# Attention by tiles: six polynomial exps per group instead of five, their squares on GpSimd, and the loads of the next group in another order

## The chip, the cores and the metric

The kernel runs on one NeuronCore of a Trainium2 chip. Its engines work side by side, each through its own instructions in order: TensorE (PE; its weight loads are listed as PEld), VectorE (DVE), ScalarE (ACT), GpSimd (POOL) and SyncE (SP), which here only issues DMA transfers. The metric is the device time of one execution in microseconds (us), as a median over runs.

## The reference

A graph network of four layers on 3327 nodes of width 128. Everything that is changed here lies in the first layer, an attention with 128 heads of width 8 over all pairs of nodes, with the adjacency matrix added twice as a bias:

```python
q = (x @ Wq.T).reshape(d, n, h)      # d = 128 heads, n = 3327 nodes, h = 8
k = (x @ Wk.T).reshape(d, n, h)
v = (x @ Wv.T).reshape(d, n, h)
a = jnp.einsum('dnh,dmh->dnm', q, k) * scale
a = a + spatial_encoding + edge_encoding          # both are adj
a = jax.nn.softmax(a, axis=2)
out = jnp.einsum('dnm,dmh->dnh', a, v)
```

So 128 x 3327 x 3327 exponentials are taken, 1.4 thousand million. The other three layers multiply the same adjacency matrix by matrices of width 128; the change does not touch them.

## The kernel before, in words

**Tiling.** Scores stand transposed, keys on the partitions. The queries are cut into 7 chunks `c` of 476 (the last 472); the 128 heads into 32 groups `g` of 4; the keys into 26 tiles of 128, taken two by two as 13 pairs `q`. One *pair* `u` is thus (chunk, group, pair of key tiles): 7 x 32 x 13 = 2912 pairs in 224 groups, and each pair makes 4 heads x 2 key tiles = 8 tiles of 128 x 476 scores.

**Steps.** The loop `for i in range(-4, 4 * n + 15)` has four steps to a pair. At step i ScalarE's exp of one head (`exps(u, j)`) stands: head j of pair u comes at i = 4u + 3j, so that four pairs are in flight. At every odd i TensorE gets a *batch*: the scores of the heads due at steps i + 1 and i + 2 (two key tiles each, so 4 matmuls, L654), then four heads' products with the values for one key tile (`values`, L713; each is two matmul instructions in the profile, so 8). So there are two batches to a pair and 26 to a group.

**Scores in place.** A score tile keeps its PSUM bank for all four heads. VectorE first writes adj - shift into it (`seed`, L645); TensorE adds head 0's scores; ScalarE reads exp(2 x) of it (L666 both key tiles at once, 952 columns, or L669 one of 476 where the two banks aren't neighbours); then TensorE adds k1 q1 - k0 q0, and so on. For that `QS` holds, for each head, its q beside the negated q of the head before. The seven banks of `S` go round, so a seed must wait until ScalarE has read the fourth head of the pair that held the bank before.

**Exps by hand.** In the pairs with q in `BY_HAND = (0, 2, 5, 7, 10)`, VectorE makes the exp of head 0's second key tile in place of ScalarE. This tile isn't seeded: its matmul starts the bank with the bare product. `hand_exp` scales it into `h` (L691), seeds the bank for head 1, and then evaluates a polynomial in three steps (L695) and a last one that multiplies by `EA` = exp(2 (adj - shift)) (L697). `EA` is made once per chunk for each q of `BY_HAND` by a subtraction (L678) and a ScalarE exp (L683). The steps of this generator are drawn one by one in the main loop, and `heads_of` lets the product with the values of such a tile come one pair later.

**Loads.** In pair q = 1 of each group the SP queue gets the 16 transfers of the next group's keys (`load_k`, L551), the 6 of its first q (`load_q`, L562 and L564), and the values (`load_v`, L575). At q = 3, 5, 7 GpSimd negates a q over all 128 partitions (L570), and the next q is loaded over half of that (6 transfers; 9 for head 1, which is also wanted in `QZ`). At q = 8 GpSimd spreads the values into `VA` (L580) and runs `all_here` (L584), a copy that reads a column of every key row; the first scores of the next group wait for it. At most eight SP transfers are outstanding, because the ninth waits for the semaphore of the first.

**Beside it.** adj for later chunks is transposed behind the attention in 22 squares of 128 rows; each takes four groups for loading (L283, q = 0), two half turns on VectorE (L288, q = 4 and 9) and a row maximum (L292, q = 12), and in a fifth group its maxima go out and back through HBM (`gather` at q = 0, L299; `back` at q = 1, L304), a bound is formed (q = 7) and 1.66 MB of transposed adj are stored (`store`, L295, q = 8). GpSimd also carries the four stores of each group's result (L725), which wait for VectorE's copy (L721).

**Start of the stage.** The SP queue gets the first values, keys, first q, shift, other q's, and then the 26 tiles of adj.

Of the kernel before, what the change touches and what calls it, by code (L numbers as in the profile page):

```python
# [10 lines left out]
F32 = mybir.dt.float32  # L11
# [6 lines left out]
ALU = mybir.AluOpType  # L18
# [4 lines left out]
P = 128  # L23
N = 3327
D = 128
H = 8
HD = D * H
NT = 26
NP = NT * P
NQ = NT // 2  # L30
# [6 lines left out]
CW = 476  # L37
# [8 lines left out]
NOTHING = -1.0e30  # L46


EXP_C = (0.9999990463256836, 2.2162604331970215, 2.4563632011413574, 1.8291265964508057)
EXP_ARG = 0.9023826718330383  # L50
BY_HAND = (0, 2, 5, 7, 10)
LN_EPS = 1e-5
L1_EPS = 1e-7
L1_MAX_TANH = 1.0 - 1e-6
# [34 lines left out]
def gnn_kernel(ctx: ExitStack, tc: tile.TileContext, x, adj, Wq, Wk, Wv, Wo, embed, layer,  # L89
               embed_bias, layer_bias, weight, bias, W_in, W_out, out):  # L90
    nc = tc.nc
# [14 lines left out]
    kS_d = dram.tile([2, H, HEADS, NP], F32, name="kS_d")  # L106
# [418 lines left out]
    with tc.tile_pool(name="e1", bufs=1) as e1, tc.tile_pool(name="e_adj", bufs=28) as e_adj, \  # L525
# [12 lines left out]
        S = e_ps.tile([P, 7, 512], F32, name="S")  # L538
        po = e_ps.tile([P, 512], F32, name="po")

        def load_k(c, g):

            b = (c * NG + g) % 2
            for j in range(4):
                d = 4 * g + j
                k0, nk = max(0, j - 1), 1 if j in (0, 3) else 2
                for r in range(2):
                    r0 = 64 * r + 32 * (1 - j % 2)
                    k_d = kS_d[:, :, d, r * NQ * P:(r + 1) * NQ * P].rearrange("i e n -> (i e) n")
                    for i in range(2):  # L550
                        nc.sync.dma_start(KT[b][r0 + 16 * i:r0 + 16 * i + 16, k0:k0 + nk, :].bitcast(F32),  # L551
                                          k_d.unsqueeze(1).to_broadcast([16, nk, NQ * P]))

        def load_q(c, g, j):

# [11 lines left out]
        def negate_q(c, g, j):  # L567

            b, w = (c * NG + g) % 2, width_of(c)
            nc.gpsimd.tensor_scalar(QS[b][:, j + 1, :w], QS[b][:, j, :w].bitcast(F32),  # L570
                                    -1.0, 0.0, op0=ALU.mult, op1=ALU.add)

        def load_v(c, g):
            v = e2.tile([P, 4, NT * H], F32, name="VR", bufs=1)
# [24 lines left out]
        with tc.If(loose < 1), tc.manual_schedule():  # L599
# [39 lines left out]
            def bank(u, r):  # L639
                return S[:, banks(u)[r], :width_of(pairs[u][0])]  # L640
# [19 lines left out]

            def exps(u, j):
                w, (even, odd) = width_of(pairs[u][0]), banks(u)
                e = e_of[u, j] = e_e.tile([P, 2, CW], F32, name=f"e{j}", bufs=(5, 4, 3, 2)[j])
                hand = j == 0 and by_hand(u)
                if even > odd and not hand:
                    touch(u, (0, 1), nc.scalar.activation(e[:, :, :w], S[:, odd:even + 1, :w], AF.Exp, scale=2.0))  # L666
                    return
                for r in range(1 if hand else 2):
                    touch(u, [r], nc.scalar.activation(e[:, 1 - r, :w], bank(u, r), AF.Exp, scale=2.0))  # L669

            def by_hand(u):

                return 0 <= u < n and pairs[u][2] in BY_HAND

            def shifted(c, q):

                w = width_of(c)
                nc.vector.tensor_tensor(EA[q][:, :w], adj_of[c][2 * q + 1][:, :w], shift_of[c][:, :w], op=ALU.subtract)  # L678

            def bare(c, q):  # L680

# [3 lines left out]
            def hand_exp(u):  # L685


                w = width_of(pairs[u][0])
                s = e_h.tile([P, CW], F32, name="h")[:, :w]
                e = e_of[u, 0][:, 0, :w]  # L690
                touch(u, [1], nc.vector.tensor_scalar(s, bank(u, 1), EXP_ARG, None, op0=ALU.mult))  # L691
                seed(u, 1)
                yield
                for k in (3, 2, 1):
                    nc.vector.scalar_tensor_tensor(e, s if k == 3 else e, EXP_C[k], s, op0=ALU.add, op1=ALU.mult)  # L695
                    yield
                nc.vector.scalar_tensor_tensor(e, e, EXP_C[0], EA[pairs[u][2]][:, :w], op0=ALU.add, op1=ALU.mult)  # L697

            def heads_of(u, r):


                first = (u, r)
                if by_hand(u) and r == 1:
                    first = (u + 1, 0)
                elif by_hand(u - 1):
                    first = (u, 1) if r == 0 else (u - 1, 1)
                return [first] + [(u, r)] * 3

            def values(u, r):
                c, g, q = pairs[u]  # L710
                w, k = width_of(c), c * NG + g
                for j, (v, of) in enumerate(heads_of(u, r)):
                    nc.tensor.matmul(po[32 * j:32 * j + H + 1, :w], VA[k % 2][:, 2 * pairs[v][2] + of, j, :],  # L713
                                     e_of[v, j][:, 1 - of, :w], start=(q == 0 and r == 0),
                                     stop=(q == NQ - 1 and r == 1))

            def store(u):
# [9 lines left out]
            def loads(u):  # L727

                c, g, q = pairs[u]
                k = c * NG + g  # L730
                if k + 1 < NC * NG:
                    nxt = divmod(k + 1, NG)
                    if q == 1:
                        load_k(*nxt)
                        load_q(*nxt, 0)
                        v_of[k + 1] = load_v(*nxt)
                    if q in (3, 5, 7):
                        negate_q(*nxt, q // 2 - 1)
                        load_q(*nxt, q // 2)
                    if q == 8:  # L740
                        spread_v(*nxt, v_of.pop(k + 1))
                        here[k + 1] = all_here(*nxt)
                if c + 1 < NC and (g, q) == (0, 0):
                    plan_squares(c)
                if g == NG - 1 and c + 1 < NC:
                    if q == 0:
                        shift_of[c + 1] = load_shift(c + 1)
                        adj_of[c + 1] = []
                    while len(adj_of[c + 1]) < min(NT, 2 * q + 6):
                        adj_of[c + 1].append(load_adj(c + 1, len(adj_of[c + 1])))  # L750


# [2 lines left out]
            def plan(u, f, *a):  # L755
                behind.setdefault(u, []).append((f, a))

            def plan_squares(c):
                for k, s in enumerate(range(squares_of(c), squares_of(c + 1))):
                    sq, u = Square(e_t, s), (c * NG + 7 * k + 1) * NQ  # L760
                    for j in range(4):
                        plan(u, sq.load, j)
                        plan(u + 4, sq.turn, j, 0)
                        plan(u + 9, sq.turn, j, 1)
                        plan(u + 12, sq.largest, j)
                        u += NQ
                    for k, f in ((0, sq.gather), (1, sq.back), (7, sq.finish), (8, sq.store)):
                        plan(u + k, f)

            v0 = load_v(0, 0)  # L770
            load_k(0, 0)
            load_q(0, 0, 0)
            shift_of[0] = load_shift(0)
            for j in range(3):
                negate_q(0, 0, j)
                load_q(0, 0, j + 1)
            spread_v(0, 0, v0)
            here[0] = all_here(0, 0)
            adj_of[0] = [load_adj(0, t) for t in range(NT)]

            for c in range(NC):
                for q in BY_HAND:
# [13 lines left out]
            for i in range(-4, 4 * n + 15):  # L796
                u, j = in_slot(i)
                if 0 <= u < n:
                    exps(u, j)
                at = i % 4  # L800
                if i == -4:
                    seed(0, 0)
                if at == 0 and by_hand(i // 4):
                    by_vector.append(hand_exp(i // 4))
                    next(by_vector[-1])
                for k in range(0 if at % 3 else 1 if at else 0 if by_hand(i // 4) else 2):
                    if by_vector and next(by_vector[0], True):
                        by_vector.popleft()
                if at == 0 and i >= 0:
                    for f, a in behind.pop(i // 4, ()):  # L810
                        f(*a)
                if at == 1 and (i + 3) // 4 < n and not by_hand((i + 3) // 4):
                    seed((i + 3) // 4, 1)
                u = (i - 14) // 4
                if at == 2 and 0 <= u < n and pairs[u][2] == NQ - 1:
                    store(u)
                if at == 2 and (i + 6) // 4 < n:
                    seed((i + 6) // 4, 0)
                if at % 2:
                    for k in (1, 2):  # L820
                        u, j = in_slot(i + k)
                        if 0 <= u < n:
                            scores(u, j)
                    u, r = ((i - 11) // 4, 0) if at == 3 else ((i - 13) // 4, 1)
                    if 0 <= u < n:
                        values(u, r)
                if at == 0 and 0 <= i // 4 < n:
                    loads(i // 4)
# [678 lines left out]
```

## Time and profile before

| | us |
|---|---|
| median of 3 runs | 10980.69 (10976.75 to 10984.85) |
| the profiled execution, whole | 10981.96 |
| the profiled execution, span on the core | 10980.2 |
| first scores of the attention / last product with the values | 461 / 10170 |
| a group of 13 pairs, median of 224 | 43.16 |

In the span from 461 to 10171 us the profile has TensorE busy for 9613.05 us, ScalarE 9669.34, VectorE 7787.13 and GpSimd 1290.03, of 9710; the granted TensorE clock there is 1.00, and the 16 DMA engines are busy for 58%.

How to read it: "busy" is the time in which an instruction of the engine is recorded as running. Successive instructions of ScalarE overlap in the record (a mean of 1099 ns for 952 columns, while they follow each other every 845 ns at best), so a busy ScalarE may still be waiting for part of it. In the rows of groups, the line stands first, then engine, operation, output<-inputs, shapes and count, then busy time and mean duration, then the idle time before them and what ended it. In the timeline each row is a start, a duration, engine, line, operation and count; equal neighbours are merged.

### The profile page before, as it was taken

The numbers are of one execution on the slowest core, as the hardware profiler recorded it, in microseconds if no ns is written. First come the engines' busy times: TensorE is split into PE (matmuls) and PEld (weight loads), VectorE is DVE, ScalarE is ACT, GpSimd is POOL, SyncE is SP. The second block draws the span as 40 slices with busy tenths as digits, with TensorE's granted clock in tenths as the row PEclk, the third lists the DMA queues.
The fourth block names the chain that finished last, engine by engine and source line by source line (L and its number), as shares of the span: only waits on it lengthen the run. The fifth ranks groups of instructions, "written<-read, shape, count | busy, mean of one in ns | idle before, by whom it ended". The sixth has DMA issues, their size and how long they took to land. (4 is left out here: it accounts for less than half of the span.)

```text
span 10980.2 us, 204474 instructions
## 1 busy us (share of the span) xinstructions
PE 10533.5 (96%) x72876; PEld 3435.7 (31%) x72876; DVE 8487.1 (77%) x13503; ACT 10033.1 (91%) x13789; POOL 1529.1 (14%) x2477
## 2 busy tenths in 40 slices
PE   4599999999999999999999999999999999999889
PEld 2133333333333333333333333333323333333544
DVE  5588887888878887788887888878877777777655
ACT  3599999999999999999999999999999999999330
POOL 5011111111111111111111111111111111111101
PEclk7799999999999999999999999999999999999999
DMA  8766566565566565565556565565556555554668
GB/s 250 250 99 97 94 96 113 93 98 96 89 118 97 93 97 88 106 98 97 90 95 119 94 96 93 95 119 95 87 93 98 96 95 86 82 88 71 206 233 281
DMA packets 695339, 1256.98 MB, mean 114 GB/s; under 512 B 195218, under 2 KB 555049, under 8 KB 691244
## 3 DMA queue, kind: packets, MB, share of 16 engines
q1 hardware_dynamic: 644044, 1114.42, 55.7%
q0 software_dynamic: 50272, 129.37, 4.3%
q8 instruction: 587, 9.62, 0.4%
q14 instruction: 436, 3.57, 0.2%
HBM read 1096.53 MB, written 146.60 MB: 113 GB/s over the span
## 5 line engine op out<-in xcount | busy, mean ns | idle before, releaser
L666 ACT ACTIVATE e<-S 128x952 f32<-128x952 f32 (+1 forms) x9024 | 8357.9, 1099 | 36.7 <-PE S L654 29.4
L713 PE MATMUL po<-e,VA 128*9 128x476 f32 (+1 forms) x46592 | 5737.5, 564 | 33.0 <-DVE OS L721 12.3
L645 DVE TENSOR_TENSOR S<-a,shb 128x476 f32<-128x476 f32 (+1 forms) x5824 | 3937.9, 676 | 1447.6 <-ACT e L666 1059.4
L654 PE MATMUL S<-QS,KT 64*128 64x476 f32 (+1 forms) x22176 | 4528.6, 445 | 79.7 <-DMA a<-adjT 28.4
L654 PEld LDWEIGHTS S<-QS,KT 64*128 64x128 f32 x22176 | 2073.7, 184 | 5100.5 <-issue 1301.3
L669 ACT ACTIVATE e<-S 128x476 f32<-128x476 f32 (+1 forms) x4128 | 2467.5, 711 | 1.1 <-PE S L654 0.6
L695 DVE SCALAR_TENSOR_TENSOR e<-e,h 128x476 f32<-128x476 f32 (+1 forms) x2240 | 1497.8, 669 | 77.0
L713 PEld LDWEIGHTS po<-e,VA 128*9 128x9 f32 x46592 | 691.0, 88 | 1606.6 <-issue 1488.1
L570 POOL TENSOR_SCALAR QS<-QS 128x476 fp32r<-128x476 f32 (+1 forms) x672 | 485.6, 723 | 4312.1 <-DMA QS<-qS_d 2612.2
L725 POOL DMA_DIRECT2D oT_d<-OS x896 | 470.5, 530 | 3668.8 <-DVE OS L721 3625.5
L691 DVE TENSOR_SCALAR h<-S 128x476 f32<-128x476 f32 (+1 forms) x1120 | 728.0, 650 | 300.9 <-PE S L654 296.5
L697 DVE SCALAR_TENSOR_TENSOR e<-e,EA 128x476 f32<-128x476 f32 (+1 forms) x1120 | 759.6, 678 | 0.0
L695 DVE SCALAR_TENSOR_TENSOR e<-h 128x476 f32<-128x476 f32 (+1 forms) x1120 | 743.1, 663 | 0.0
L1107 PE MATMUL pu<-strip,y 128*128 128x512 f32 (+2 forms) x1456 | 600.5, 566 | 31.7 <-DVE y L968 14.8
L654 PE MATMUL S<-QZ,KT 64*128 64x476 f32 (+1 forms) x1120 | 493.4, 441 | 11.9 <-DVE S L645 10.5
L1107 PEld LDWEIGHTS pu<-strip,y 128*128 128x128 f32 (+1 forms) x1456 | 271.9, 191 | 305.8 <-issue 272.1
L1111 DVE TENSOR_REDUCE deg<-strip 128x1 f32<-128x1536 f32 (+1 forms) x104 | 193.8, 1881 | 63.7 <-DMA strip<-adjT 44.1
L580 POOL COPY VA<-VR 128x832 f32<-128x832 f32 x224 | 242.3, 1082 | 0.0
L654 PEld LDWEIGHTS S<-QZ,KT 64*128 64x128 f32 x1120 | 205.1, 183 | 92.2 <-DVE S L645 52.4
L288 DVE STREAM_TRANSPOSE cols<-rows 128x416 f32<-128x416 f32 x208 | 204.5, 988 | 30.3 <-DMA rows<-in_adj_dram 22.6
L1060 ACT COPY uT<-pu 128x512 f32<-128x512 f32 (+1 forms) x21 | 11.1, 555 | 222.6 <-PE pu L1107 222.6
L721 DVE COPY OS<-po 128x476 f32<-128x476 f32 (+1 forms) x224 | 146.3, 653 | 87.3 <-PE po L713 87.3
(255 smaller groups left out, 1958.6 us busy)
## 6 DMA issues: line engine op xcount, KB each, us to landing
KT<-kS_d SPq DMA_DIRECT2D x1792, 208.0 KB
KT<-kS_d SPq DMA_DIRECT2D x1792, 104.0 KB
VR<-v_d SPq DMA_DIRECT2D x224, 416.0 KB
QS<-qS_d SPq DMA_DIRECT2D x3072, 14.9 KB
QS<-qS_d SPq DMA_DIRECT2D x1536, 29.8 KB
adjT<-cols SPq DMA_DIRECT2D x26, 1664.0 KB
a<-adjT SPq DMA_DIRECT2D x156, 238.0 KB
strip<-adjT POOLq DMA_DIRECT2D x39, 895.5 KB, 5.1
```

The lines of the kernel that those rows point to most:

```text
L570: nc.gpsimd.tensor_scalar(QS[b][:, j + 1, :w], QS[b][:, j, :w].bitcast(F32), -1.0, 0.0, op0=ALU.mult, op1=ALU.add)
L580: nc.gpsimd.tensor_copy(VA[(c * NG + g) % 2][:, :, :, 0:H], v.rearrange("p j (t e) -> p t j e", e=H))
L645: touch(u, [r], nc.vector.tensor_tensor(bank(u, r), adj_of[c][2 * q + r][:, :w], shift_of[c][:, :w], op=ALU.subtract))
L654: x = nc.tensor.matmul(bank(u, r), KT[b][64 * r:64 * r + 64, max(0, j - 1), q * P:(q + 1) * P], q_s[64 * r:64 * r + 64, :w], start=hand an ...
L666: touch(u, (0, 1), nc.scalar.activation(e[:, :, :w], S[:, odd:even + 1, :w], AF.Exp, scale=2.0))
L669: touch(u, [r], nc.scalar.activation(e[:, 1 - r, :w], bank(u, r), AF.Exp, scale=2.0))
L691: touch(u, [1], nc.vector.tensor_scalar(s, bank(u, 1), EXP_ARG, None, op0=ALU.mult))
L695: nc.vector.scalar_tensor_tensor(e, s if k == 3 else e, EXP_C[k], s, op0=ALU.add, op1=ALU.mult)
L697: nc.vector.scalar_tensor_tensor(e, e, EXP_C[0], EA[pairs[u][2]][:, :w], op0=ALU.add, op1=ALU.mult)
L713: nc.tensor.matmul(po[32 * j:32 * j + H + 1, :w], VA[k % 2][:, 2 * pairs[v][2] + of, j, :], e_of[v, j][:, 1 - of, :w], start=(q == 0 and r ...
L725: nc.gpsimd.dma_start(oT_d[:, d * N + c * CW:d * N + c * CW + w], o[32 * j:32 * j + H + 1, :w])
L1107: nc.tensor.matmul(ps[:, :k], y[:m, t, :], s[:m, c * 4 * P - c0:c * 4 * P - c0 + k], start=(t == 0), stop=(t == NT - 1))
```

## The change

It does five things.

1. `BY_HAND` becomes (0, 2, 4, 6, 8, 10). The polynomial is another one of the same degree: z = s + c0 on VectorE, z z on **GpSimd** (128 x 476, a new line), then z' = (zz + c1) + z, e = (zz + c2) z' and e = (e + c3) EA on VectorE. That is four VectorE instructions and one on GpSimd in place of five on VectorE. The constant that the polynomial leaves out goes into `shifted`.
2. The generator is drawn at other steps: none at step 3 of the pair itself, two at the next step 0, one at the next step 3. `heads_of` is gone: each product with the values comes with its own pair. `e0` has 4 buffers instead of 5.
3. All four q's of the next group are loaded at q = 1, ahead of the keys; the negations write only the two blocks of 32 partitions that hold the q (two instructions of 32 partitions each) and come at q = 5, 7, 9. The values are loaded at q = 3, and spread and `all_here` come at q = 12.
4. Squares: loads at q = 3, turns at q = 10 and 12, `store` at q = 2 of the fifth group (before: q = 8); adj tiles of the next chunk are asked for one pair later.
5. At the start of the stage: the q's, the shift and four tiles of adj, then the keys, the values, and the other 22 tiles.

```diff
-BY_HAND = (0, 2, 5, 7, 10)
+BY_HAND = (0, 2, 4, 6, 8, 10)
...
+            for r0 in (32 * (1 - j % 2), 64 + 32 * (1 - j % 2)):
+                nc.gpsimd.tensor_scalar(QS[b][r0:r0 + 32, j + 1, :w], QS[b][r0:r0 + 32, j, :w].bitcast(F32),
+                                        -1.0, 0.0, op0=ALU.mult, op1=ALU.add)
...
-                touch(u, [1], nc.vector.tensor_scalar(s, bank(u, 1), EXP_ARG, None, op0=ALU.mult))
+                touch(u, [1], nc.vector.tensor_scalar(z, bank(u, 1), EXP_C[0], None, op0=add))
+                nc.gpsimd.tensor_tensor(e, z, z, op=mult)
                 seed(u, 1)
                 yield
-                for k in (3, 2, 1):
-                    nc.vector.scalar_tensor_tensor(e, s if k == 3 else e, EXP_C[k], s, op0=ALU.add, op1=ALU.mult)
-                    yield
-                nc.vector.scalar_tensor_tensor(e, e, EXP_C[0], EA[pairs[u][2]][:, :w], op0=ALU.add, op1=ALU.mult)
+                v(z, e, EXP_C[1], z, op0=add, op1=add)
+                yield
+                v(e, e, EXP_C[2], z, op0=add, op1=mult)
+                yield
+                v(e, e, EXP_C[3], EA[pairs[u][2]][:, :w], op0=add, op1=mult)
...
                     if q == 1:
-                        load_k(*nxt)
-                        load_q(*nxt, 0)
+                        for j in range(4):
+                            load_q(*nxt, j)
+                        for j in range(4):
+                            load_k(*nxt, j)
+                    if q in (5, 7, 9):
+                        negate_q(*nxt, q // 2 - 2)
+                    if q == 3:
                         v_of[k + 1] = load_v(*nxt)
-                    if q in (3, 5, 7):
-                        negate_q(*nxt, q // 2 - 1)
-                        load_q(*nxt, q // 2)
-                    if q == 8:
+                    if q == 12:
                         spread_v(*nxt, v_of.pop(k + 1))
                         here[k + 1] = all_here(*nxt)
...
-                        plan(u, sq.load, j)
-                        plan(u + 4, sq.turn, j, 0)
-                        plan(u + 9, sq.turn, j, 1)
+                        plan(u + 3, sq.load, j)
+                        plan(u + 10, sq.turn, j, 0)
+                        plan(u + 12, sq.turn, j, 1)
                         plan(u + 12, sq.largest, j)
                         u += NQ
-                    for k, f in ((0, sq.gather), (1, sq.back), (7, sq.finish), (8, sq.store)):
+                    for k, f in ((0, sq.gather), (1, sq.back), (2, sq.store), (7, sq.finish)):
                         plan(u + k, f)
...
-                for k in range(0 if at % 3 else 1 if at else 0 if by_hand(i // 4) else 2):
+                for k in range(0 if at % 3 or by_hand(i // 4) else 1 if at else 2):
```

More of the change, by code (lines that the diff above doesn't have):

```diff
@@ L46 @@
 NOTHING = -1.0e30
-EXP_C = (0.9999990463256836, 2.2162604331970215, 2.4563632011413574, 1.8291265964508057)
-EXP_ARG = 0.9023826718330383
-BY_HAND = (0, 2, 5, 7, 10)
+EXP_C = (0.25674915313720703, 0.05050157010555267, 1.8002841472625732, 0.8117094039916992)
+EXP_LEAD = -0.2054332047700882
+BY_HAND = (0, 2, 4, 6, 8, 10)
 LN_EPS = 1e-5
@@ L539, in gnn_kernel, with load_k @@
         po = e_ps.tile([P, 512], F32, name="po")
-        def load_k(c, g):
+        def load_k(c, g, j):
             b = (c * NG + g) % 2
[L544 to L552, printed above, removed]
+            d = 4 * g + j
+            k0, nk = max(0, j - 1), 1 if j in (0, 3) else 2
+            for r in range(2):
+                r0 = 64 * r + 32 * (1 - j % 2)
+                k_d = kS_d[:, :, d, r * NQ * P:(r + 1) * NQ * P].rearrange("i e n -> (i e) n")
+                for i in range(2):
+                    nc.sync.dma_start(KT[b][r0 + 16 * i:r0 + 16 * i + 16, k0:k0 + nk, :].bitcast(F32),
+                                      k_d.unsqueeze(1).to_broadcast([16, nk, NQ * P]))
         def load_q(c, g, j):
@@ L569, in negate_q @@
             b, w = (c * NG + g) % 2, width_of(c)
-            nc.gpsimd.tensor_scalar(QS[b][:, j + 1, :w], QS[b][:, j, :w].bitcast(F32),
-                                    -1.0, 0.0, op0=ALU.mult, op1=ALU.add)
+            for r0 in (32 * (1 - j % 2), 64 + 32 * (1 - j % 2)):
+                nc.gpsimd.tensor_scalar(QS[b][r0:r0 + 32, j + 1, :w], QS[b][r0:r0 + 32, j, :w].bitcast(F32),
+                                        -1.0, 0.0, op0=ALU.mult, op1=ALU.add)
         def load_v(c, g):
@@ L662, in exps @@
                 w, (even, odd) = width_of(pairs[u][0]), banks(u)
-                e = e_of[u, j] = e_e.tile([P, 2, CW], F32, name=f"e{j}", bufs=(5, 4, 3, 2)[j])
+                e = e_of[u, j] = e_e.tile([P, 2, CW], F32, name=f"e{j}", bufs=(4, 4, 3, 2)[j])
                 hand = j == 0 and by_hand(u)
@@ L677, in shifted @@
                 w = width_of(c)
-                nc.vector.tensor_tensor(EA[q][:, :w], adj_of[c][2 * q + 1][:, :w], shift_of[c][:, :w], op=ALU.subtract)
+                nc.vector.scalar_tensor_tensor(EA[q][:, :w], adj_of[c][2 * q + 1][:, :w], EXP_LEAD, shift_of[c][:, :w],
+                                               op0=ALU.add, op1=ALU.subtract)
             def bare(c, q):
@@ L688, in hand_exp @@
                 w = width_of(pairs[u][0])
-                s = e_h.tile([P, CW], F32, name="h")[:, :w]
+                v, add, mult = nc.vector.scalar_tensor_tensor, ALU.add, ALU.mult
+                z = e_h.tile([P, CW], F32, name="h")[:, :w]
                 e = e_of[u, 0][:, 0, :w]
-                touch(u, [1], nc.vector.tensor_scalar(s, bank(u, 1), EXP_ARG, None, op0=ALU.mult))
+                touch(u, [1], nc.vector.tensor_scalar(z, bank(u, 1), EXP_C[0], None, op0=add))
+                nc.gpsimd.tensor_tensor(e, z, z, op=mult)
                 seed(u, 1)
                 yield
-                for k in (3, 2, 1):
-                    nc.vector.scalar_tensor_tensor(e, s if k == 3 else e, EXP_C[k], s, op0=ALU.add, op1=ALU.mult)
-                    yield
-                nc.vector.scalar_tensor_tensor(e, e, EXP_C[0], EA[pairs[u][2]][:, :w], op0=ALU.add, op1=ALU.mult)
[L699 to L707, printed above, removed]
+                v(z, e, EXP_C[1], z, op0=add, op1=add)
[3 more added lines that the diff above has]
+                v(e, e, EXP_C[3], EA[pairs[u][2]][:, :w], op0=add, op1=mult)
             def values(u, r):
@@ L711, in values @@
                 w, k = width_of(c), c * NG + g
-                for j, (v, of) in enumerate(heads_of(u, r)):
-                    nc.tensor.matmul(po[32 * j:32 * j + H + 1, :w], VA[k % 2][:, 2 * pairs[v][2] + of, j, :],
-                                     e_of[v, j][:, 1 - of, :w], start=(q == 0 and r == 0),
+                for j in range(4):
+                    nc.tensor.matmul(po[32 * j:32 * j + H + 1, :w], VA[k % 2][:, 2 * q + r, j, :],
+                                     e_of[u, j][:, 1 - r, :w], start=(q == 0 and r == 0),
                                      stop=(q == NQ - 1 and r == 1))
@@ L733, in loads @@
                     if q == 1:
-                        load_k(*nxt)
-                        load_q(*nxt, 0)
+                        for j in range(4):
+                            load_q(*nxt, j)
+                        for j in range(4):
+                            load_k(*nxt, j)
+                    if q in (5, 7, 9):
+                        negate_q(*nxt, q // 2 - 2)
+                    if q == 3:
                         v_of[k + 1] = load_v(*nxt)
-                    if q in (3, 5, 7):
-                        negate_q(*nxt, q // 2 - 1)
-                        load_q(*nxt, q // 2)
-                    if q == 8:
+                    if q == 12:
                         spread_v(*nxt, v_of.pop(k + 1))
@@ L748, in loads @@
                         adj_of[c + 1] = []
-                    while len(adj_of[c + 1]) < min(NT, 2 * q + 6):
+                    while len(adj_of[c + 1]) < min(NT, 2 * q + 4):
                         adj_of[c + 1].append(load_adj(c + 1, len(adj_of[c + 1])))
@@ L761, in plan_squares @@
                     for j in range(4):
-                        plan(u, sq.load, j)
-                        plan(u + 4, sq.turn, j, 0)
-                        plan(u + 9, sq.turn, j, 1)
+                        plan(u + 3, sq.load, j)
+                        plan(u + 10, sq.turn, j, 0)
+                        plan(u + 12, sq.turn, j, 1)
                         plan(u + 12, sq.largest, j)
                         u += NQ
-                    for k, f in ((0, sq.gather), (1, sq.back), (7, sq.finish), (8, sq.store)):
+                    for k, f in ((0, sq.gather), (1, sq.back), (2, sq.store), (7, sq.finish)):
                         plan(u + k, f)
+            for j in range(4):
+                load_q(0, 0, j)
+            shift_of[0] = load_shift(0)
+            adj_of[0] = [load_adj(0, t) for t in range(4)]
+            for j in range(4):
+                load_k(0, 0, j)
             v0 = load_v(0, 0)
-            load_k(0, 0)
-            load_q(0, 0, 0)
-            shift_of[0] = load_shift(0)
+            adj_of[0] += [load_adj(0, t) for t in range(4, NT)]
             for j in range(3):
                 negate_q(0, 0, j)
-                load_q(0, 0, j + 1)
             spread_v(0, 0, v0)
             here[0] = all_here(0, 0)
-            adj_of[0] = [load_adj(0, t) for t in range(NT)]
             for c in range(NC):
```

## The prediction

> **What bounds the kernel now.** I read the busy row first, then the groups, then the timeline of one pair by hand. 461 to 10171 us is the attention; nothing else is changed, so only those 9710 us are argued about.
>
> ```profile
> PE 10533.5 (96%) x72876; PEld 3435.7 (31%) x72876; DVE 8487.1 (77%) x13503; ACT 10033.1 (91%) x13789; POOL 1529.1 (14%) x2477
> ...
> L666 ACT ACTIVATE e<-S 128x952 f32<-128x952 f32 (+1 forms) x9024 | 8357.9, 1099 | 36.7 <-PE S L654 29.4
> L645 DVE TENSOR_TENSOR S<-a,shb 128x476 f32<-128x476 f32 (+1 forms) x5824 | 3937.9, 676 | 1447.6 <-ACT e L666 1059.4
> L691 DVE TENSOR_SCALAR h<-S 128x476 f32<-128x476 f32 (+1 forms) x1120 | 728.0, 650 | 300.9 <-PE S L654 296.5
> ```
>
> TensorE and ScalarE both look full. ScalarE's idle of 36.7 us hides waits, because its records overlap. From start to start, an exp of 952 columns takes 0.845 us at best and one of 476 takes 0.447; times the counts (9024, and 4128 in L669) that is 9460 us, 42.23 a group. The median group takes 43.16. TensorE's batches start 1.54 us apart at best (5th percentile in non-hand pairs), 26 x 1.54 = 40.04 a group. So the two are close, and what ties them is VectorE, in the pairs by hand:
>
> ```profile
> 5012.88 0.87 PE L654 MATMUL S<-QS,KT 64*128 64x476 f32 x4
> ...
> 5013.42 0.65 DVE L691 TENSOR_SCALAR h<-S 128x476 f32<-128x476 f32 x1 [0.37 <-PE S L654]
> ...
> 5014.11 0.66 DVE L645 TENSOR_TENSOR S<-a,shb 128x476 f32<-128x476 f32 x1
> ...
> 5014.83 0.18 PEld L654 LDWEIGHTS S<-QZ,KT 64*128 64x128 f32 x1
> 5014.92 0.39 PE L654 MATMUL S<-QZ,KT 64*128 64x476 f32 x1
> ...
> 5015.48 1.43 DVE L645 TENSOR_TENSOR S<-a,shb 128x476 f32<-128x476 f32 x2 [0.71 <-ACT e L666]
> ```
>
> The reader should see a chain: scores of head 0 (5012.88), scaling, seed, scores of head 1 (5014.92): 2.04 us, also the median. Head 1 stands 0.33 us into the next batch, so that batch can't start earlier than 1.71 after the first: 0.17 over the floor for each pair by hand. Two more losses show in the medians of the batch starts: 0.22 where the first values of a group wait for the result copy (L721), and 0.61 in the first batch of pair 4 (2.15 us), whose seed stands behind that copy and three polynomial steps. TensorE's path is thus 40.04 + 5 x 0.17 + 0.22 + 0.61 = 41.72, under ScalarE's 42.23, and the group takes 0.93 more than the larger.
>
> **The change part by part.** I sum against the profiled execution, 10982.0 us (span 10980.2), 1.3 over the median of 10980.7.
>
> *ScalarE.* One more pair by hand in each of 224 groups. In 6 of 7 the banks are neighbours: 192 exps go from 952 to 476 columns, and in 32 one of two 476s falls away: -192 x 0.398 - 32 x 0.447 = -90.7 us. Seven more `EA` (L683, 0.49 from start to start) give back 3.4: -87.3, or 41.84 a group.
>
> *VectorE.* Four instructions x 6 instead of five x 5: 24 for 25, each 0.65. It had 1447.6 us of idle before its seeds; I take the saved instruction at nothing. Pair 4 by hand needs no seed of its second tile there, which takes the 0.61 away. `shifted` with one constant more has the shape of L678: nothing, 7 instructions.
>
> *GpSimd's squares.* 128 x 476, two inputs. The nearest rows are adds of two tiles in the first stage; the line through them gives 1268 - 36 x 2.13 ns = 1.19 us.
>
> ```profile
> L369 POOL TENSOR_TENSOR sq<-sq 128x512 f32<-128x512 f32 x52 | 65.9, 1268 | 28.5 <-ACT sq L367 27.4
> L369 POOL TENSOR_TENSOR sq<-sq 128x256 f32<-128x256 f32 x52 | 37.6, 722 | 4.2
> ```
> ```profile
> 5001.89 0.88 POOL L580 COPY VA<-VR 128x832 f32<-128x832 f32 x1
> ...
> 5002.44 0.84 DVE L645 TENSOR_TENSOR S<-a,shb 128x476 f32<-128x476 f32 x1 [0.54 <-ACT e L666]
> 5002.71 0.61 POOL L584 COPY seen<-KT 128x3 f32<-128x3 f32 x1
> ```
>
> The square itself is hidden: scaling ends at 5014.07, the first polynomial step is at 5016.82 and now comes a step later, 2.75 us for 1.19. Without that cover VectorE would stand for what is left, and the seeds behind it, and TensorE with them. Its price is what the second extract shows: a seed of 0.66 us takes 0.84 while GpSimd works. Over the attention, GpSimd's negations overlap VectorE by 0.57 us and stretch it by 0.187, a third. The square starts some 0.14 us after the scaling ends and covers 0.52 of the seed on the chain: 0.17 us. Bounds: nothing, as GpSimd was on no chain and can't shorten one (in the first stage the adds overlap VectorE for 0.66 us and stretch it by 0.016), and 0.36 (149 seeds wholly covered take 1.017). I take 0.17, since the negations run beside these very seeds.
>
> The Trainium skill, "SBUF — State Buffer", section "SBUF: two separate sides", says that a VectorE instruction with two SBUF inputs and a GpSimd one that reads SBUF exclude each other for the whole instruction. By that rule a seed behind the square could wait all of 1.19 us, TensorE's path would be 48.4 and the time about 12,490 (an estimate); the third seen in this trace speaks for far less.
>
> *TensorE's path after:* 40.04 + 6 x (0.17 + 0.17) + 0.22 = 42.30, now over ScalarE's 41.84. With the same 0.93 on top 43.23: +0.07 x 224 = +16 us. With 0 ScalarE is the larger: 42.77, -87. With 0.36: 44.37, +271.
>
> *Values with their own pair, narrow negations.* A product with the last polynomial comes four steps earlier, but still five steps (over 4 us) after the step that draws it: nothing. If a step slipped that far, TensorE would wait in order. Six negations of 32 partitions for three of 128 (0.72 us each, at worst the same) add 2.2 us to an engine with 14% busy; their q's are loaded four pairs ahead: nothing.
>
> *Loads.* Ordinary groups: 27 q transfers at 0.35 us issue in 9.4, the keys begin that much later. Keys now end 18.9 us (median) after a point 2.1 us past the group's first scores, values at 22.3; some 10 us later both are still 9 us ahead of the check. Nothing. What is late is a group with a `store`:
>
> ```profile
> 5141.41 1.75 SPq L299 DMA_DIRECT2D rowmax_d<-rm  x4
> 5150.48 0.38 SPq L304 DMA_DIRECT2D four<-rowmax_d  x1
> 5150.96 12.74 SPq L551 DMA_DIRECT2D KT<-kS_d  x16
> ...
> 5186.22 0.53 SPq L295 DMA_DIRECT2D adjT<-cols  x1
> 5189.90 15.81 SPq L551 DMA_DIRECT2D KT<-kS_d  x16
> ```
>
> There `back` waits for the maxima to land, so SP's queue is free only at 5150.9. After: the row maximum comes behind a turn, +1.0; 27 q's to 5161.3; keys 20.5 (this group's took 22.0, with q's between; 18.8 to 23.2 in the 22 such groups) to 5181.8; now the store is in front of the values in the queue. Its packets last 7.5 (6.2 from 3328 packets x 29.7 ns on 16 engines, up to 10.5 from issue to end), the values 2: 5191.3. That transfers on this queue follow one another shows in the keys issued at 5189.90: their first packet runs at 5193.6, when the store's are nearly through. L580 and L584 (0.9 + 0.6) end at 5192.8; the next group's first scores stood at 5185.5 and wait for L584: 7.3 late. This group's keys began 1.1 later than the median of the 22: 6.2, less 0.4 that TensorE is ahead of ScalarE: 5.8 x 22 = +128 us. Bounds: 50 (keys 18.8, store 6.2, values 1.6) and 262 (23.2 and 10.5). In a chunk's last group, adj tiles stand in front of the values too: by the same sum about level with the first scores, nothing, at most 2 us x 6.
>
> *Squares' other moves.* A turn of 0.99 us now shares pair 10 with a polynomial, in 88 groups; nothing, at most 0.3 each, 26 us. GpSimd's memset of the rows then waits only for loads a group older.
>
> *Start.* First ScalarE work is at 460.7, behind adj. After: q's 9.4, shift and four tiles 2.7 from 419.8, keys 16.8 to 448.7, landed and values in by 452.5, spread and check to 453.7: -7.
>
> Sum: 10982 + 16 + 128 - 7 = **11119**.
>
> **Rivals.** *ScalarE's gain passes, values late:* the squares cost under 0.09 us, where TensorE's path falls below 41.84: 10982 - 87 + 128 - 7 = 11016. For: stage one's adds; against: the 0.84 seed. *Faster: ScalarE sets the group again.* One mechanism, in every group: the 0.39 us that it saves come off whole, -87; it decides where the squares cost under those 0.09 us and late values under 3.3 us a store (22 x 3.3 = 72). For: keys at their 18.8 and the shortest store come near that (2.3). Against: the SP rows above. With no late values: 10888. *Squares block the seeds:* 0.36 on the chain: 10982 + 271 + 128 - 7 = 11374. For: the 149 covered seeds; against: their partner was mostly the longer copy. *The squares don't run where written,* held up on GpSimd behind a wait: against it, loads precede the negations by four pairs, and only L725 waits for VectorE (3625.5 us of idle), at pair 2 behind that pair's square; it would look like the blocked seeds.
>
> **How the numbers follow.** Forecast 0.45 (own range 11040 to 11210), gain with late values 0.21, faster 0.20, blocked or held squares 0.14. 10890 to 11330 leaves out about half of each of the last two. This kernel's runs spread by 0.07%, and 0.2% is 22 us. Faster: 0.18 of the third case and 0.03 of the second, should its late values cost half; same: 0.02 and 0.05 of these two; slower: the rest, 0.72.
>
> **What would show it.** Rows of 1344 squares near 1.2 us; L666 at 8832. Right: idle of TensorE's loads before L654 put down to L584 or L580, 22 times, 4 to 8 us; seeds (L645) above a mean of 0.70; ScalarE's starts further apart than 0.845 more often. Wrong: groups under 42.9 us, no wait at the stores, or the values landing before the store's packets end.

## The result, and the profile after

| | before | after |
|---|---|---|
| median, us | 10981.1 (4 runs, 10976.8 to 10984.9) | 11117.0 (4 runs, 11113.6 to 11125.3) |
| span of the profiled execution | 10980.2 | 11115.3 |
| start of the attention | 461.2 | 453.5 |
| the 22 groups with a `store`, sum | 950.6 | 1101.4 |
| the 6 last groups of a chunk, sum | 268.4 | 323.7 |
| the 194 other groups between, sum (median of one) | 8393.3 (43.15) | 8330.6 (42.61) |

The ratio is 1.0124, 95% interval 1.0112 to 1.0137. The forecast was 11119, 2 us away, but the table shows that it is not right line by line. A group is the time from its first scores to the next group's; both columns add up the same groups. The differences are -7.7, +150.8, +55.3 and -62.8, with +0.8 in the first and the last group: +136.4 of the span's +135.1. The forecast had -7, +128, nothing, and +16 in all groups.

The busy row and the groups of the page after, with the same columns as before:

```profile
PE 10500.9 (94%) x72876; PEld 3475.3 (31%) x72876; DVE 8815.9 (79%) x13286; ACT 9929.7 (89%) x13764; POOL 4117.5 (37%) x4493
...
L666 ACT ACTIVATE e<-S 128x952 f32<-128x952 f32 (+1 forms) x8832 | 8328.9, 1140 | 81.8 <-PE S L654 79.4
...
L645 DVE TENSOR_TENSOR S<-a,shb 128x476 f32<-128x476 f32 (+1 forms) x5824 | 4310.8, 740 | 1333.9 <-ACT e L666 973.4
...
L694 POOL TENSOR_TENSOR e<-h 128x476 f32<-128x476 f32 (+1 forms) x1344 | 1828.5, 1360 | 5170.5 <-DVE h L693 4176.2
...
L570 POOL TENSOR_SCALAR QS<-QS 32x476 fp32r<-32x476 f32 (+1 forms) x1344 | 1191.2, 886 | 99.5 <-DMA QS<-qS_d 5.6
```

L694 is the square, 1344 times as forecast, at 1.36 us instead of 1.19. L570, the negation, takes 0.89 us on 32 partitions, where it took 0.72 on 128, and there are twice as many. The seeds (L645) rose from 676 to 740 ns. All three means contain waits of VectorE and GpSimd for each other, which later sections sort out.

The waits of the kernel after (which instruction waits for which; total us, times, longest) name both losses:

```profile
PEld S L654 <- POOL seen L584: 202.3, 23, 20.7
...
DVE EA L678 <- DMA a<-adjT: 64.5, 7, 13.8
```

The first is the arrival check ahead of a group's first scores, 23 times: once at the start of the attention (20.7 us) and at the 22 groups with a store. One of these groups in the timeline of the kernel after, SP's queue first:

```profile
5242.73 12.42 SPq L550 DMA_DIRECT2D KT<-kS_d  x16
5256.60 0.54 SPq L295 DMA_DIRECT2D adjT<-cols  x1
5258.40 8.64 SPq L575 DMA_DIRECT2D VR<-v_d  x1
...
5271.28 0.88 POOL L580 COPY VA<-VR 128x832 f32<-128x832 f32 x1 [12.54 <-DMA VR<-v_d]
5272.10 0.19 POOL L584 COPY seen<-KT 128x3 f32<-128x3 f32 x1
...
5272.34 0.77 PEld L654 LDWEIGHTS S<-QS,KT 64*128 64x128 f32 x4 [7.15 <-POOL seen L584]
...
5273.70 1.77 PE L707 MATMUL po<-e,VA 128*9 128x476 f32 x8
...
5276.49 1.75 PE L707 MATMUL po<-e,VA 128*9 128x476 f32 x8
...
5278.80 0.99 PE L707 MATMUL po<-e,VA 128*9 128x476 f32 x8
```

The store is issued at 5256.60, the values right behind it, and GpSimd gets them at 5271.28: TensorE's weight loads stand for 7.15 us. The chain is the forecast's, link by link. Then follows what it did not have: eight products with the values, 0.99 us elsewhere, take 1.77 and 1.75. The windows view of the same place (length; busy time and count of PE, PEld, DVE, ACT and POOL; the granted TensorE clock; the DMA share and GB/s) says why:

```profile
5270.00:5272.30 2.30, 0.00 (x0) 0.00 (x0) 0.00 (x0) 0.00 (x0) 1.01 (x2) 0.50 0.59 43
5272.30:5278.70 6.40, 6.36 (x28) 1.82 (x28) 4.43 (x6) 3.35 (x4) 1.38 (x1) 0.55 0.16 26
5278.70:5290.00 11.30, 11.17 (x86) 3.46 (x84) 8.36 (x13) 11.28 (x17) 4.32 (x6) 1.00 0.64 111
```

The clock has fallen to 0.50 while TensorE stood, and it is 1.00 again only some 6 us after work began. A stop is paid twice.

The second wait is at the end of a chunk, again in the timeline after:

```profile
6074.55 12.99 SPq L550 DMA_DIRECT2D KT<-kS_d  x16
...
6088.95 5.07 SPq L590 DMA_DIRECT2D a<-adjT  x4
...
6096.97 0.65 DVE L678 SCALAR_TENSOR_TENSOR EA<-a,shb 128x476 f32<-128x476 f32 x1 [8.10 <-DMA a<-adjT]
6097.66 0.60 ACT L684 ACTIVATE EA<-EA 128x476 f32<-128x476 f32 x1 [6.41 <-DVE EA L678]
```

`shifted` for q = 2 of the next chunk stands eight pairs ahead of its use and needs adj tile 5. In the kernel before, six adj tiles were asked for ahead of the keys. Now only four are (part 4 of the change asks one pair later), so tile 5 is queued behind 27 q and 16 key transfers and lands 8.10 us late; VectorE, in order, makes no seed meanwhile, and ScalarE stands behind it.

### The profile page after: what moved, and what is told of

Same layout as the page of the kernel before. It is cut to its first block, busy times and chain, and to the rows that moved or that the text cites. A ratio compares the mean times of both kernels' runs of the same rounds, so it can differ in the third digit from the quotient of the medians.

```text
span 11115.3 us, 205876 instructions
## 1 busy us (share of the span) xinstructions
PE 10500.9 (94%) x72876; PEld 3475.3 (31%) x72876; DVE 8815.9 (79%) x13286; ACT 9929.7 (89%) x13764; POOL 4117.5 (37%) x4493
## 3 DMA queue, kind: packets, MB, share of 16 engines
q8 instruction: 581, 9.52, 0.4%
## 4 chain that ended last, share of the span: by engine, by line
ACT 41%; PE 40%; issue 7%; DMA 3%; DVE 3%; SPq 2%; POOL 0%; DVEq 0%; POOLq 0%; ACTq 0%
ACT e L666 33%; PE po L707 20%; PE S L654 15%; ACT e L669 7%; PE pu L1105 5%; DMA KT<-kS_d 1%; SPq L575 1%; DVE S L645 1%; DMA QS<-qS_d 1%; DVE OS L715 1%; SPq L550 0%; DMA a<-adjT 0%; PE pu L1186 0%; DVE h L693 0%; DMA adjT<-cols 0%
## 5 line engine op out<-in xcount | busy, mean ns | idle before, releaser
L645 DVE TENSOR_TENSOR S<-a,shb 128x476 f32<-128x476 f32 (+1 forms) x5824 | 4310.8, 740 | 1333.9 <-ACT e L666 973.4
L654 PE MATMUL S<-QS,KT 64*128 64x476 f32 (+1 forms) x21952 | 4463.0, 448 | 212.3 <-POOL seen L584 120.9
L694 POOL TENSOR_TENSOR e<-h 128x476 f32<-128x476 f32 (+1 forms) x1344 | 1828.5, 1360 | 5170.5 <-DVE h L693 4176.2
L669 ACT ACTIVATE e<-S 128x476 f32<-128x476 f32 (+1 forms) x4288 | 2690.8, 755 | 177.4 <-PE S L654 177.0
L570 POOL TENSOR_SCALAR QS<-QS 32x476 fp32r<-32x476 f32 (+1 forms) x1344 | 1191.2, 886 | 99.5 <-DMA QS<-qS_d 5.6
L697 DVE SCALAR_TENSOR_TENSOR h<-e,h 128x476 f32<-128x476 f32 (+1 forms) x1344 | 1120.5, 834 | 0.0
L693 DVE TENSOR_SCALAR h<-S 128x476 f32<-128x476 f32 (+1 forms) x1344 | 871.1, 648 | 264.1 <-PE S L654 253.3
L699 DVE SCALAR_TENSOR_TENSOR e<-e,h 128x476 f32<-128x476 f32 (+1 forms) x1344 | 879.0, 654 | 46.1
L701 DVE SCALAR_TENSOR_TENSOR e<-e,EA 128x476 f32<-128x476 f32 (+1 forms) x1344 | 868.8, 646 | 0.0
L654 PE MATMUL S<-QZ,KT 64*128 64x476 f32 (+1 forms) x1344 | 612.3, 456 | 51.6 <-DVE S L645 51.3
L580 POOL COPY VA<-VR 128x832 f32<-128x832 f32 x224 | 279.7, 1249 | 331.2 <-DMA VR<-v_d 268.4
L288 DVE STREAM_TRANSPOSE cols<-rows 128x416 f32<-128x416 f32 x208 | 205.1, 991 | 32.2 <-DMA rows<-in_adj_dram 24.2
```

Of the source, the lines that this page charges most:

```text
L570: nc.gpsimd.tensor_scalar(QS[b][r0:r0 + 32, j + 1, :w], QS[b][r0:r0 + 32, j, :w].bitcast(F32), -1.0, 0.0, op0=ALU.mult, op1=ALU.add)
L645: touch(u, [r], nc.vector.tensor_tensor(bank(u, r), adj_of[c][2 * q + r][:, :w], shift_of[c][:, :w], op=ALU.subtract))
L654: x = nc.tensor.matmul(bank(u, r), KT[b][64 * r:64 * r + 64, max(0, j - 1), q * P:(q + 1) * P], q_s[64 * r:64 * r + 64, :w], start=hand an ...
L693: touch(u, [1], nc.vector.tensor_scalar(z, bank(u, 1), EXP_C[0], None, op0=add))
L694: nc.gpsimd.tensor_tensor(e, z, z, op=mult)
L697: v(z, e, EXP_C[1], z, op0=add, op1=add)
```

## The experiments

None of the eleven kernels leaves out any of the work. "With both repairs" means the changed kernel with the second and third edits below.

**The store, from two sides.** First the store alone is put back:

```diff
-                    for k, f in ((0, sq.gather), (1, sq.back), (2, sq.store), (7, sq.finish)):
+                    for k, f in ((0, sq.gather), (1, sq.back), (7, sq.finish), (8, sq.store)):
```

> The changed kernel with one thing undone: the store of the transposed squares is planned at pair 8 of its group again, so that the next group's values stand ahead of it in SP's queue. Theory: the 22 groups with a store took 1101.4 us, and at an ordinary group's 42.94 they would take 944.7, so -157; the groups behind them stand 1.1 us over a mean before, so up to -25 more: 10935 to 10965 us, store groups at 43 to 44 us each. The forecast's own sum for this wait (5.8 us x 22): -128, 10989. Rival, that the stores' traffic or the turns beside them make these groups long wherever the values stand: within 30 us of 11117.

Measured: 10951.5 us; store groups 972.1. Then the store stays and the values go ahead of it:

```diff
                         for j in range(4):
                             load_k(*nxt, j)
+                        v_of[k + 1] = load_v(*nxt)
...
-                    if q == 3:
-                        v_of[k + 1] = load_v(*nxt)
```

> The changed kernel with the values loaded at pair 1, right behind the keys, instead of at pair 3; the store stays at pair 2 and now follows them in SP's queue. Theory (only the order of values and store matters): as with the store planned late, 10935 to 10965 us. Rival, that the early store harms by its place beside the keys: well above that, 11000 to 11117.

Measured: 10932.2 us, 3 under the range; store groups 950.9, as in the kernel before. So 166 us (by moving the store) to 185 (by moving the values; 8.4 a store) hang on which of two transfers stands first in one queue, and little on the store's place or traffic. With the store put back, five of its groups still take 45 to 49 us: in one, the values are issued at 5151.08 and the store at 5154.45, and the values reach GpSimd only at 5166.72. Why a store behind the values still delays them there, and hardly with the values at pair 1, was not followed further.

**The chunk's end.**

```diff
-                        plan(u - (8 if c else 2), shifted, c, q)
-                        plan(u - (7 if c else 1), bare, c, q)
+                        plan(u - (4 if c else 2), shifted, c, q)
+                        plan(u - (3 if c else 1), bare, c, q)
```

> The changed kernel with EA of the next chunk made 4 and 3 pairs ahead of its use instead of 8 and 7, nothing else. Theory: at the six chunk boundaries VectorE stands in order at L678 for an adj tile that is now queued behind 27 q and 16 key transfers; four pairs later (some 13 us, the wait was 8.1) the tile is there, and the six groups lose their 55 us: 11050 to 11075 us, boundary groups at 43 to 46 us instead of 54. Rival, that the adj tiles are late for the seeds themselves: the wait moves from L678 to L645 and the boundary groups stay at 50 us or more, 11095 to 11120.

Measured: 11048.3 us, 69 less and 2 under the range. The six groups fall from 323.7 to 259.2, 43.2 each, while the six behind them rise from 44.2 to 46.3. Four of the six `EA` subtractions and exps now fall there, instead of two: two exps of 0.49 are 1.0 of these 2.1 us, and where the rest comes from was not followed. L678 waits for an adj tile once, at the start of the attention, instead of 7 times, so the seeds weren't late. By the profiles the boundaries give 52 of the 69 (64.5 less 12.8); the rest lies in groups that the edit doesn't touch.

**Both repairs at once.**

> The changed kernel with values at pair 1 and EA made late, both at once; candidate to beat both kernels. Theory (two separate waits that add): 10932 less the 69 that the late EA alone brought = 10863, 10850 to 10880 us, that is, the kernel before less ScalarE's gain and the start. Rival, that one wait hides behind the other: 10890 or more.

Measured: 10882.0 us, ratio to the kernel before 0.9914 (0.9901 to 0.9928). It beats both kernels. It misses its range by 2 us, within the spread of its five runs (10869.1 to 10889.2); the profiled execution's span is 10867.3. The two repairs gave 235 together and 254 one by one.

**The exps alone.** The kernel before gets the new exps, and nothing of the loads, negations, turns and stores.

```diff
-BY_HAND = (0, 2, 5, 7, 10)
+BY_HAND = (0, 2, 4, 6, 8, 10)
...
+                nc.gpsimd.tensor_tensor(e, z, z, op=mult)
...
-                for k in range(0 if at % 3 else 1 if at else 0 if by_hand(i // 4) else 2):
+                for k in range(0 if at % 3 or by_hand(i // 4) else 1 if at else 2):
```

> The kernel before with the exps alone changed: six pairs by hand, the new polynomial with its square on GpSimd, each product with its own pair; all loads, negations, turns and stores as before. Theory (ScalarE's gain passes, the square costs nothing on the chain): 0.54 us off each of 224 groups, -121: 10840 to 10880 us. Recorded forecast (TensorE's path takes over, stretched by the squares): +16, 10990 to 11005. Rival, that squares block the seeds: 11250 or more.

Measured: 13018.7 us, ratio 1.186. My theory and the recorded forecast missed. The time lies in the rival's open range, but not by the rival's overlap of square and seed. The timeline of this kernel shows the mechanism:

```profile
6131.54 0.59 POOL L570 TENSOR_SCALAR QS<-QS 128x476 fp32r<-128x476 f32 x1 [11.73 <-DMA QS<-qS_d]
6132.10 0.97 POOL L694 TENSOR_TENSOR e<-h 128x476 f32<-128x476 f32 x1
...
6133.10 0.66 DVE L697 SCALAR_TENSOR_TENSOR h<-e,h 128x476 f32<-128x476 f32 x1 [9.02 <-POOL e L694]
```

GpSimd waits 11.73 us for a q that is queued behind the keys. In the kernel before nobody minded, since GpSimd had nothing else to do. Now pair 4's square stands behind the negation, VectorE's polynomial waits 9.02 us for the square, and the seeds stand behind the polynomial. The batch that waits there, in pair 6, starts 9.52 us after the one before it (median) instead of 1.66, in every group. If that is the cause, one instruction moved off GpSimd ends it:

```diff
-                nc.gpsimd.tensor_tensor(e, z, z, op=mult)
                 seed(u, 1)
+                nc.vector.tensor_tensor(e, z, z, op=mult)
```

> The exps alone changed, as in the run that took 13018 us, with the square on VectorE instead of GpSimd and nothing else. Theory (the 2040 us come from GpSimd's order: each square stands behind a negation at pairs 3, 5 and 7 that waits for a q queued behind the keys, and VectorE's polynomial, and the seeds behind it, wait for the square): they vanish, 10860 to 11000 us. Rival, that six pairs by hand with these draw steps need more of VectorE than it has, or that the q's come late for TensorE itself: 12000 or more.

Measured: 10950.0 us; 2069 us gone. Which part of the new load order frees GpSimd? Three kernels, each with both repairs, differ in two lines: the loop over `load_k` ahead of the loop over `load_q` (the first), negations at q = 3, 5, 7 (the second), both (the third).

```diff
-                    if q in (5, 7, 9):
-                        negate_q(*nxt, q // 2 - 2)
+                    if q in (3, 5, 7):
+                        negate_q(*nxt, q // 2 - 1)
```

> Both repairs, with the 16 key transfers ahead of the 27 q's in SP's queue again; negations stay at pairs 5, 7, 9. Theory (only GpSimd's order matters): the first q lands some 17 us behind pair 1 (12.9 of key issue, 2.1 of its own, 2 to land), its negation is due after 13, so the square of pair 6 starts some 2.5 us late against 1.4 of slack: 0 to 1.2 us a group, 10880 to 11150 us. Rival, that the keys' place costs by itself as much as in the run with the exps alone: over 12000.

> Both repairs, with the negations at pairs 3, 5, 7 as in the kernel before; the q's stay ahead of the keys. Theory: the first q has landed some 4.5 us behind pair 1 and the negation is due after 6.6, so nothing on GpSimd waits: 10865 to 10900 us, as with both repairs. Rival, that a negation at pair 3 holds up the square of pair 4 by its own 1.8 us: up to 0.5 us a group, to 10995.

> Both repairs, with the keys ahead of the q's and the negations at pairs 3, 5, 7 at once, as in the kernel before. Theory: the negation due 6.6 us behind pair 1 waits till 17, GpSimd stands with it, the square of pair 4 is some 7 us late, and TensorE, which then stands over 2 us, runs at half speed for 5 us more: 7 to 10 us a group, 12450 to 13100 us, the loss of the run with the exps alone. Rival, that this loss had another source (full-width negations, the other q's loaded late): under 11300.

Measured: 11290.6, 10909.1 and 12964.7 us. Keys first costs 409, more than the 268 I allowed: the late square is pair 6's as said (TensorE's second batch in pair 8 comes 2.78 us after the first, not 1.66), but in the 22 store groups, where the queue begins late, the group takes 53.5 us instead of 43.2, which is 226 of the 409. There GpSimd waits 14.4 us a group for q's, and VectorE 9.1 for squares. Early negations cost 27, over the first range and inside the rival's. Both together cost 2083: q's ahead of the keys or late negations, either one alone, avoid most of the loss, so the two costs are not a sum.

**What the square costs, and the sixth pair.** With both repairs, the square goes to VectorE (the same edit as above):

> Both repairs, with the square on VectorE, behind the seed of the same step, instead of on GpSimd. Theory (the square costs nothing on GpSimd, and VectorE has 1344 x 0.65 = 874 us more to do): 10870 to 10990 us, no faster than with both repairs. Recorded forecast's term (each square on GpSimd stretches the seed beside it by 0.17 us, 6 a group, 228 us on TensorE's path): faster than with both repairs by 20 us or more.

Measured: 11045.5 us, 163 slower; the recorded term had the wrong sign, and my theory's range ended 55 us short. The ordinary group takes 43.53 us instead of 42.60. Most of it arises in pairs 4 and 5, where two batches start 1.98 and 2.11 us after the ones before them (medians) instead of 1.72 and 1.56. The timeline there, of this kernel and then of the one with both repairs:

```profile
5003.57 5.33 POOL L570 TENSOR_SCALAR QS<-QS 32x476 fp32r<-32x476 f32 x6
5004.02 0.65 DVE L693 TENSOR_SCALAR h<-S 128x476 f32<-128x476 f32 x1
5004.71 0.90 DVE L645 TENSOR_TENSOR S<-a,shb 128x476 f32<-128x476 f32 x1
5005.53 1.02 DVE L695 TENSOR_TENSOR e<-h 128x476 f32<-128x476 f32 x1
```
```profile
5008.68 0.65 DVE L693 TENSOR_SCALAR h<-S 128x476 f32<-128x476 f32 x1
5009.36 0.66 DVE L645 TENSOR_TENSOR S<-a,shb 128x476 f32<-128x476 f32 x1
5009.50 1.35 POOL L694 TENSOR_TENSOR e<-h 128x476 f32<-128x476 f32 x1 [1.34 <-DVE h L693]
...
5010.95 1.82 POOL L570 TENSOR_SCALAR QS<-QS 32x476 fp32r<-32x476 f32 x2
```

Both extracts show a seed (L645) on the chain of a pair by hand. In the lower one it starts 0.14 us ahead of the square and takes 0.66 us. In the upper one it starts inside a negation and takes 0.90, and all six negations come in one run of 5.33 us, because no square stands between them on GpSimd: in the changed kernel the squares, which wait for VectorE, also hold each pair of negations back to a place behind the chain. The same seed, pair 4's, has a median of 0.94 here, 0.90 with early negations and 0.66 with both repairs. With early negations the same batch of pair 4, the one behind the batch that waits for this seed, comes 1.98 us after the one before it, again instead of 1.72, so this is what they cost.

Last, five pairs by hand again, `BY_HAND = (0, 2, 5, 7, 10)`, with both repairs:

> Both repairs, with BY_HAND back at (0, 2, 5, 7, 10) and everything else as changed. Theory (ScalarE sets the ordinary group and its gain passed): the sixth pair was worth 87 us by ScalarE's records and 120 by the groups, so 10950 to 10985 us, ordinary groups at 43.0 to 43.2. Rival, that the shorter groups came from the loads or the late negations and not from the sixth pair: within 30 us of the kernel with both repairs.

Measured: 10950.9 us, at the low end of the range. The sixth pair is worth 69 us (80 between the profiled spans), somewhat less than the 87 to 120 expected; the ordinary group has a median of 43.02 against 42.60.

## Why the prediction was right in the number and not in its steps

- **Start, -7:** measured -7.7. Right.
- **Late values, +128 (22 x 5.8):** mechanism right, size too small: 185 by the runs, 8.4 a store. TensorE stands 7.4 us on average at these ends (4.1 to 11.0) where the sum had 6.2. The rest fits the clock: two batches of products at 1.77 instead of 0.99 are 1.6 us, less what TensorE catches up. Neither rise was in the sum, which had TensorE resume at full speed.
- **ScalarE, -87.3, "not seen", and TensorE's path, +16:** wrong. The failed step is "0.17 us" for the seed beside the square. Its geometry was exact: in the trace after, the square starts 0.17 us after the scaling's end (forecast 0.14) and covers 0.52 of the seed (0.52). But 1337 of the 1344 seeds on the chain of a pair by hand stand beside their square and take 0.661 us on average, as those beside nothing do. The true price was the lower bound, nothing, because this seed starts ahead of the square. What comes first keeps its time and the other waits: the square is the longer one, 1.36 us instead of the 0.97 that it takes alone. The rows show both sides:

```profile
509.26 0.64 DVE L693 TENSOR_SCALAR h<-S 128x476 f32<-128x476 f32 x1
...
509.94 0.66 DVE L645 TENSOR_TENSOR S<-a,shb 128x476 f32<-128x476 f32 x1
510.05 1.38 POOL L694 TENSOR_TENSOR e<-h 128x476 f32<-128x476 f32 x1 [5.23 <-DVE h L693]
...
510.82 1.13 DVE L645 TENSOR_TENSOR S<-a,shb 128x476 f32<-128x476 f32 x1 [0.22 <-ACT e L669]
```

  The seed at 509.94 is ahead of the square and takes 0.66. The next one, at 510.82, starts inside it and takes 1.13; it is on no chain of a pair by hand. The third that I took from the negations is a mean over seeds on both sides of that line, and a mean can't price the one seed that counts. The adds of the first stage, which pointed to nothing, are no better a witness: the VectorE instructions beside them (copies and a subtraction out of PSUM, turns and row maxima) read at most one tensor from SBUF, and such instructions don't wait for GpSimd in these traces (last section). With nothing for the square, the sum's own path for TensorE is 41.28, under ScalarE's 41.84, and the sixth pair passed: in the trace after, a pair by hand takes TensorE 3.28 to 3.37 us from its first batch to the next pair's (medians by pair), exactly as in the trace before; the sum had added 0.17. The rival "gain passes, values late" (11016) had the true outcome here, and missed in the size of the losses.
- **The sign that deceived:** I had named a mean of L645 above 0.70 as proof. It is 0.740. Of the 459 us behind that rise, 237 come from seeds that start inside a square, 122 inside a negation and 99 inside the copy that spreads the values, and none from the seeds on the chain that are beside a square. So the squares do lengthen seeds, 0.20 us each for 1173 of them, but not where TensorE waits. Groups under 42.9 us, named as disproof, are there: 42.61. A mean over unlike cases was a poor witness; the seeds should have been sorted by which instruction starts first.
- **A chunk's last group, "nothing, at most 2 us x 6":** wrong, 55 us in these groups, 69 by the run. I asked only whether the values behind the adj tiles come in time, not who else waits for these tiles: `shifted`, eight pairs ahead, with VectorE's seeds behind it. The step "every queue that it is moved past" was made for SP's values and left out for its adj.
- **Loads in ordinary groups, "nothing":** true of TensorE's wait, but the reason missed what the order is for. It makes GpSimd free for the squares. "Held up on GpSimd behind a wait" was listed as a rival and excluded by "loads precede the negations by four pairs": right for the changed kernel, and the runs show that 2083 us hang on it.

So three errors met: about 107 too dear in the exps (a forecast of +16, against some -91 in 10882.0 less 10981.1 and the start), and 57 and 69 too cheap in the waits (107 together, as the two repairs give 235 and not 254). They cancel by luck, and the number proves nothing about the sum.

Two rules of the Trainium skill can be set against these rows. "SBUF — State Buffer", section "SBUF: two separate sides", has a VectorE operation with two SBUF inputs and a GpSimd one that reads SBUF exclude each other: whichever starts first has the port pair for the whole instruction. The runs agree, with their numbers in the last section. The prediction drew 12,490 us from this rule by letting the square come first; on the chain the seed does, and then the rule costs the square 0.39 us and the seed nothing. "TensorE: Matmul & The Clock Gate", section "HAM oscillation — how this bites in real kernels", warns of idle gaps of TensorE over about 3.4 us; the runs here agree, with an earlier edge (last section).

## What to carry to other kernels

An idle engine that works in order may hide long waits at no cost; before work that others wait for is put on it, look up what its instructions already wait for. When a load is moved in a queue, list every reader of everything behind it, on all engines, not only the reader you had in mind. And before an overlap of VectorE and GpSimd is priced, look up in the trace which of the two instructions starts first: a seed ahead of a square lost nothing here, and one inside it 0.20 us on average.

## What the runs showed of the hardware

- **TensorE's clock after a stop.** Over the traces of both kernels and all experiments, I took every stop of TensorE in the attention and looked for a batch of products over 1.4 us (0.99 is usual) in the 8 us behind it. After stops of 1 to 1.5 us there was one, before any further stop, in 6 of 104 cases, after 1.5 to 2 us in 8 of 15, after 2 to 3.4 us in 4 of 4, and after more in 547 of 547 (most of these in the two kernels that stop once a group).
- **VectorE and GpSimd wait for each other, and the one that starts first doesn't.** Over the same traces, none of 12,876 seeds that start ahead of the square or negation beside them is longer than usual. Of 16,299 that start inside one with over 0.2 us of it left, 16,290 are, and the other 9 start within 0.02 us of it. Those that are longer end 0.66 us after a point that lies 0.15 us ahead of GpSimd's end, however much of it was left. A square that starts behind a seed ends 0.83 us after the seed's end (1.36 us in all), and takes 0.97 with no seed beside it (223 times in the run with the exps alone). The polynomial's first step (L697) takes 1.03 inside a negation and 0.65 alone.
- **VectorE instructions with one input from SBUF, or none, showed no such wait:** the turn (L288) takes 1.00 us inside a square and 0.99 alone, the scaling (L693, which reads PSUM) 0.65 inside a negation and 0.65 alone.
- **Fewer partitions were not cheaper on GpSimd:** with nothing on VectorE beside it, a negation of 476 columns takes 0.58 us on 32 partitions (446 times in the run with keys first and early negations) and 0.59 on 128 (248 times in the run with the exps alone). The means of 0.89 and 0.72 differ by the waits for VectorE.
